# A pre-norm decoder layer: two pairs of FFN blocks by two levels of Winograd's products in the first pass, another order of the inner products, and the second pass's operands loaded together

## The chip, the cores and the metric

The kernel runs on one core of a Trainium2 chip. The metric is the device time of one launch in microseconds (us), for the kernel before the median of three runs. A profile of one execution accompanies it: for each instruction its engine, its start, its length and what ended the idle time ahead of it. The engines are named PE (TensorE, matrix products, with PEld for its weight loads), DVE (VectorE), ACT (ScalarE), POOL (GpSimd) and SP (SyncE, which here only issues DMAs).

## What is computed

Everything is float32. The input `x` holds 16 batches of 128 rows of 1024 numbers. Three residual steps follow one another:

```python
x = x + attention(layernorm(x))                # one head, d = 256
x = x + linear_attention(layernorm(x), ctx)    # 8 heads of 64
x = x + ffn(layernorm(x))
```

The change lies in the third:

```python
g = einsum('bsh,ih->bsi', x, Wg)     # 2048 rows x 1024 -> 2752
u = einsum('bsh,ih->bsi', x, Wu)
h = silu(g) * u
return einsum('bsi,hi->bsh', h, Wd)  # 2752 -> 1024
```

`Wg`, `Wu` and `Wd` come as packed 4-bit numbers with a scale and a zero for each group of 64; the kernel unpacks them itself.

## The kernel before

**One level.** The 2752 rows of gate and up are cut into ten blocks of 256 and a last one of 192. The 2048 rows of `x` are taken in two passes of 1024. For a block and a pass, a product of 256 x 1024 by 1024 x 1024 is cut into two by two in every dimension and made of Winograd's seven products instead of eight. Each of the seven, numbered 1 to 7, is four matmuls of 128 x 128 x 512. `one_block` (L1113) does seven for gate and seven for up, in the order `GATE` = 1, 7, 6, 2, 5, 4, 3 (L39). The left operands, the combined weights, come from DRAM; the right ones are the cut rows `T[1]` to `T[7]`.

**Two levels.** `two_levels` (L1295) takes two blocks, 2i and 2i+1, at once. For each of the seven outer products q, in the order `DOWN` = 1, 2, 6, 5, 3, 7, 4 (L40), it cuts the operands once more and does seven inner products p, each of four matmuls of 128 x 128 x 256. Four left combinations of an outer product (p = 7, 5, 6, 3) are made by GpSimd (`inner_left`, the tile `li`); four right ones (p = 7, 5, 6, 4) by VectorE (`inner_right`, the tile `ti`), each a subtraction of 128 x 512. The other operands are parts of `w` and `T[q]`. In the first pass a right combination is made for each outer product of each pair. In the second pass those of q = 1, 6, 5, 4, 7 are kept from the first pair on (`KEPT`, L1230), and q = 2 and 3 are made again in each pair.

**Sums.** Inner products 6, 5 and 3 add to the PSUM bank of product 1, and 4 to that of product 7. ScalarE copies the bank after 1, 7 and 6 (`k`). `got` (L1339) takes one quarter of an outer product out of PSUM: quarter (0,0) after product 2, (1,1) after 5, (1,0) after 4, (0,1) after 3, and adds it to the sums `U`, `V` and `C`. Quarters with a copy to add take two VectorE instructions (three for q = 7, one for q = 1), the last takes one (two for q = 7; for q = 1 a ScalarE copy). When a quarter of the pair's result is complete (q = 2, 3, 7, 4), `finish` (L1365) sets ScalarE to the SiLU of gate and leaves two VectorE products (`h`) for the next outer product, in `soon_due`.

**The order.** TensorE, VectorE and GpSimd run these parts in the order of the program text (`InOrder`, L54). The queues `right` (right combinations of the next outer product) and `extra` (combinations of the second pass's results) are worked off by `do_extra(n, more)` at fixed places. So the lines L1417 to L1461 are the order of every engine: before, one turn of the loop for outer product n had TensorE do n's 6, 2, 5, 4, then 1 of n+1, then n's 3, then 7 of n+1.

**Preparation.** `prepare` (L200) is a generator that unpacks the weights of blocks 5 to 10 and of `Wd`. One step unpacks half a matrix (two integer instructions and two float ones on VectorE, the tile `pa`) or makes four combinations (`pc`). SP loads the packed numbers (L173, L176, L192, L193) two halves ahead and stores the results (L209). `beside` (L1502) takes a number of steps after each one-level product, counted by its place n in the block; `two_levels` takes one after q = 1, 6 and 5 in the first pass; what is left is done after the last block (L1550).

**Weights and rows.** `load_weights` (L1012) keeps four tiles of two weight matrices each ahead of their use, on SP. In the first pass, blocks 0 to 5 go by one level, blocks 6 and 7 (pair 3) by two, then blocks 8 and 9 and the last block by one. The second pass does all five pairs by two levels. Its rows `T1` are loaded from DRAM by `block_loads` (L541) into memory that the two-level stage of the first pass leaves: eight loads of 512 KB on SP, one after every third product of blocks 8 and 9 (L1517). `outer_operand` (L1061) makes three right operands of the second pass during the first pass's last block, `last_block` (L1142).

Of the kernel before, what the change touches and what calls it, by code (L numbers as in the profile page):

```python
# [65 lines left out]
def decoder_layer(  # L66
# [474 lines left out]
    def block_loads(p, blocks):  # L541

        for k in ((0, 0), (1, 0), (1, 1), (0, 1)):
            for i in range(2):
                part = slice(None), ts(i, JC // 2)
                tc.keep_in_program_order(nc.sync.dma_start(blocks[k][part], xt_all[p][k][part]))
                yield
# [415 lines left out]
    with ExitStack() as gs:  # L963
# [36 lines left out]
            return [[(2 * i + f, mat, q) for mat in "gu"] for q in DOWN for f in range(2)]  # L1000


        PAIRS = [3]
        order = [blk for blk in range(RB) if blk // 2 not in PAIRS]
        order.insert(2 * PAIRS[0], None)
        to_load = deque([t for blk in order[: 2 * PAIRS[0]] for t in tiles_of(blk)])
# [288 lines left out]
        def two_levels(ps, pairs, operands, between=lambda q: None):  # L1295
# [9 lines left out]
            def do_extra(n, more=0):  # L1305
                for todo, k in ((right, n), (extra, more)):
                    for _ in range(min(k, len(todo))):
                        todo.popleft()()
# [5 lines left out]
            def multiply(n, p):  # L1314
                L, bank = state[n]["L"], state[n]["bank"]
                q = OUTERS[n][1]
                set_ = {6: 1, 5: 1, 3: 1, 4: 7}.get(p, p)
                if set_ == p:
                    bank[p] = banks[n % 2].tile([P, 2, HT], F32, name=f"q{p}", tag="gu")
                dst = bank[set_]  # L1320
                for m in range(2):
                    for c in range(CHUNKS):
                        tensor.matmul(
                            dst[:, m, :],
                            L[p][:, m, c, :],
                            R[q, p][:, c, :],

                            start=(set_ == p and m == c == 0),
                            stop=(p in (2, 3, 4) and c == CHUNKS - 1),
                            skip_group_check=True,  # L1330
                        )
                if p in (1, 7, 6):
                    t = state[n]["kept"][p] = ct.tile(
                        [P, 2, HT], F32, name="k", tag=f"k{p}", bufs=2 if p == 1 else 1
                    )
                    scalar.copy(t, dst)
                put_stores()

            def got(n, ib, p, add):  # L1339

                q = OUTERS[n][1]
                src = state[n]["bank"][p]
                add = state[n]["kept"].get(add)
                k = 2 * ib[0] + ib[1]
                add_to = vector.tensor_tensor
                U, V, C = (sums.get(x) for x in "UVC")
                if q == 1:
                    if add is None:
                        scalar.copy(U[:, k], src)
                    else:  # L1350
                        add_to(U[:, k], src, add, ALU.add)
                    return
                dst, base = {2: (C, U), 6: (U, U), 5: (V, U), 3: (C, V), 7: (C, V), 4: (C, U)}[q]
                if add is None:
                    if q == 7:
                        add_to(U[:, k], src, U[:, k], ALU.add)
                    add_to(dst[:, k], src, base[:, k], ALU.add)
                    return
                m = V if q == 5 else C
                add_to(m[:, k], src, add, ALU.add)  # L1360
                if q == 7:
                    add_to(U[:, k], U[:, k], m[:, k], ALU.add)
                add_to(dst[:, k], m[:, k], base[:, k], ALU.add)
# [47 lines left out]
            for n, (i, q) in enumerate(OUTERS):  # L1411
                last = n + 1 == len(OUTERS)
                if q in (1, 5):
                    sums["U" if q == 1 else "V"] = place.tile(
                        wide, F32, name="U" if q == 1 else "V"
                    )
                load_weights()  # L1417
                if not last:
                    prepare_outer(n + 1)
                    left = state[n + 1]["left"]  # L1420
                    left(7)
                multiply(n, 6)
                do_extra(len(right))
                while soon_due:
                    soon_due.popleft()()
                if q not in (1, 5):
                    sums["C"] = place.tile(wide, F32, name="C")
                if not last:
                    right.extend(operands.inner_right(OUTERS[n + 1][1]))
                if ps == 1 and n == 0:  # L1430
                    extra.append(lambda: outer_operand(operands.T, 4))
                elif ps == 1 and n == 4:
                    extra.extend(operands.inner_right(4))
                multiply(n, 2)
                got(n, (0, 0), 2, 1)
                multiply(n, 5)
                got(n, (1, 1), 1, 7)
                if not last:
                    left(5)
                    left(6)  # L1440
                do_extra(1, 1)
                multiply(n, 4)
                got(n, (1, 0), 7, 6)
                do_extra(1, 1)
                if not last:
                    multiply(n + 1, 1)
                    do_extra(1, 1)
                multiply(n, 3)
                got(n, (0, 1), 1, None)
                if not last:  # L1450
                    left(3)
                do_extra(0, 1)
                load_weights()

                do_extra(len(right) - 2)
                if not last:
                    multiply(n + 1, 7)
                    do_extra(len(right) - 1)
                if q in (2, 3, 7, 4):
                    finish(i, q)  # L1460
                between(q)  # L1461


                if ps == 0:
                    pass
                elif q == 3:
                    while extra:
                        extra.popleft()()
                    hl = load_first(i, 1)
                elif q == 7:  # L1470
                    soon_due.append(lambda i=i, hl=hl: combine(i, 1, hl))
                elif q == 1 and i > 0 or last:
                    while soon_due:
                        soon_due.popleft()()
                    do_extra(0, len(extra))
                    hl = load_first(i if last else i - 1, 0)
                    combine(i if last else i - 1, 0, hl)
                del state[n]
# [23 lines left out]
        def beside(n, mat, q):  # L1502
            if rest is None:
                tick()
                if not pend:
                    attention_done()
            else:

                if blk == 0:
                    steps = 1  # L1510
                elif blk == RB:
                    steps = n in (0, 2, 4)
                else:
                    steps = (1, 1 + (mat == "g" and blk < 3), 1, 0, 1, 0, 0)[n % 7]
                for _ in range(steps):
                    next(rest, None)
            if pass1 and n % 3 == 0:  # L1517
                next(pass1_loads, None)
            if blk == 2 * PAIRS[0] - 1 and n == 9:
                for step in first_operands.inner_right(DOWN[0]):  # L1520
                    step()

            if blk == RB:
                for k in {("r", 0): (5,), ("r", 1): (7,), ("m", 6): (6,)}.get((mat, q), ()):
                    outer_operand(T1, k)
                if (mat, q) == ("m", 1):
                    for step in second_operands.inner_right(1):
                        step()

        pass1 = None  # L1530
        for blk in order:
            if blk is None:
                two_levels(
                    0, PAIRS, first_operands, lambda q: q in (1, 6, 5) and next(rest, None)
                )
                deep.close()
                cxb = pool("c_xb", 1)
                pass1 = new_blocks(cxb, lambda k: f"b{k}")
                pass1_loads = block_loads(1, pass1)
                T1.update({1: pass1[0, 0], 2: pass1[1, 0], 3: pass1[1, 1]})  # L1540
                continue
            if blk == 2 * PAIRS[0] - 1:
                first_operands.pool = deep.enter_context(
                    tc.tile_pool(name="c_d", bufs=1, reuse_waits="tile")
                )
            one_block(blk, T, beside)
        blk = RB
# [282 lines left out]
```

## Time and profile before

| what | us |
|---|---|
| median of 3 runs (2287.0 to 2289.8) | 2288.38 |
| the profiled execution | 2287.6 |
| its span, first to last instruction | 2285.8 |
| TensorE busy in the span | 2258.2 |
| VectorE busy | 1600.1 |
| blocks 1 to 5, first pass, one level | 883.4 to 1123.75 |
| pair 3, first pass, two levels | 1123.75 to 1212.68 |
| blocks 8, 9 and the last one, one level | 1212.68 to 1346.58 |
| five pairs, second pass, two levels | 1346.58 to 1771.3 |

The times in the last four rows are places in the span. Each float32 matmul leaves two records, and a record's length overlaps with the next one's; what a stage costs is read from the start of its first record to the start of the next stage's first. `p` is the PSUM tile of a one-level product, `q` that of an inner product. An instruction made through `InOrder` carries the line of that helper, L62, so groups are told apart by the names of their tiles. The matmul records of product 4 are `q<-ti,w`, those of 5, 6 and 7 `q<-ti,li`, those of 3 `li` with `b` or `T`, those of 1 and 2 `w` with `b` or `T`.

### The profile page before, as it was taken

Reading aid. Unit: us, or ns where it says so; the run is one execution under the profiler, and the core shown is the slowest. Engines: PE = TensorE matmul, PEld = TensorE weight load, DVE = VectorE, ACT = ScalarE, POOL = GpSimd, SP = SyncE. Lnnn points to the kernel's source line nnn. Section 1 sums busy time; section 2 is a strip of 40 time slices with the busy share of each in tenths; the row PEclk is TensorE's granted clock in tenths of the full one; section 3 lists DMA queues with packets and bytes.
Section 4 is the critical chain, followed back from the end, with each engine's and each line's share of the span. In section 5 each row is a group of like instructions: output and inputs, shape, how many; then the busy total and the mean of one; then the engine's idle time right before and its main releaser. Section 6 shows DMA issues by size and latency. Waiting matters only on the chain.

```text
span 2285.8 us, 25587 instructions
## 1 busy us (share of the span) xinstructions
PE 2258.2 (99%) x9096; PEld 1612.5 (71%) x9096; DVE 1600.1 (70%) x2145; ACT 560.0 (24%) x893; POOL 471.8 (21%) x381
## 2 busy tenths in 40 slices
PE   8999999999999999999999999999999999999999
PEld 7556566666666664444584468888888588888888
DVE  6997788788788937666696658877777555544463
ACT  2111255665665652111111111121111100000000
POOL 5452122222222210000240024444443000000000
PEclk9999999999999999999999999999999999999999
DMA  6445366566676558877747942654554974434631
GB/s 246 158 135 182 102 166 183 158 194 185 173 230 196 169 165 269 276 261 262 242 137 232 322 137 95 202 185 139 192 196 137 331 242 151 142 124 149 222 116 37
DMA packets 270319, 425.23 MB, mean 186 GB/s; under 512 B 26224, under 2 KB 119792, under 8 KB 270064
## 3 DMA queue, kind: packets, MB, share of 16 engines
q1 hardware_dynamic: 244112, 377.71, 52.3%
q0 software_dynamic: 8064, 27.27, 3.2%
q10 hardware_dynamic: 18016, 18.62, 2.6%
q8 instruction: 73, 1.20, 0.2%
q14 instruction: 54, 0.44, 0.1%
HBM read 265.62 MB, written 157.35 MB: 185 GB/s over the span
## 4 chain that ended last, share of the span: by engine, by line
PE 91%; DVE 5%; issue 1%; DMA 1%; ACT 1%; POOL 0%; SPq 0%; DVEq 0%; POOLq 0%; ACTq 0%
PE po L1715 21%; PE q L62 20%; PE p L62 18%; PE mm L62 11%; PE kq L62 9%; PE mm L391 4%; PE tr L62 3%; PE mm L406 2%; PE p L1092 2%; DVE pa L62 1%; PE mm L287 1%; PE tr L338 1%; DVE ti L62 0%; DVE bnst L62 0%; DMA kh<-kd 0%
## 5 line engine op out<-in xcount | busy, mean ns | idle before, releaser
L62 PE MATMUL p<-b,w 128*128 128x512 f32 x560 | 246.4, 592 | 0.0
L62 PE MATMUL q<-ti,li 128*128 128x256 f32 x1008 | 232.2, 379 | 3.5 <-DVE ti L62 3.4
L62 PEld LDWEIGHTS q<-ti,li 128*128 128x128 f32 x1008 | 191.0, 190 | 31.3 <-issue 2.8
L62 POOL TENSOR_TENSOR li<-w 128x512 f32<-128x512 f32 x84 | 117.8, 1405 | 432.2 <-DMA w<-wu 244.4
L62 PEld LDWEIGHTS p<-b,w 128*128 128x128 f32 x560 | 106.4, 190 | 133.1 <-issue 129.4
L1715 PE MATMUL po<-wc,lc 128*128 128x256 f32 x840 | 183.4, 379 | 0.0
L62 PE MATMUL p<-T,w 128*128 128x512 f32 x400 | 177.2, 592 | 0.0
L709 POOL TENSOR_TENSOR qe<-qe,qden 128x1024 f32<-128x1024 f32 x64 | 121.7, 1901 | 266.5 <-DVE qden L62 244.7
L1715 PEld LDWEIGHTS po<-wc,lc 128*128 128x128 f32 x840 | 159.6, 190 | 21.8
L62 ACT COPY k<-q 128x512 f32<-128x512 f32 x126 | 73.7, 585 | 400.0 <-PE q L62 400.0
L62 PEld LDWEIGHTS p<-T,w 128*128 128x128 f32 x400 | 76.0, 190 | 95.7 <-issue 94.9
L1715 PE MATMUL po<-wq,lq 128*128 128x256 f32 x560 | 126.7, 379 | 0.4 <-issue 0.4
L62 PE MATMUL mm<-kh,cxt 128*128 128x256 f32 x512 | 122.6, 382 | 3.2 <-DMA kh<-kd 2.8
L62 PEld LDWEIGHTS mm<-qs,m_sb 128*128 128x128 f32 x512 | 97.2, 190 | 38.9 <-issue 28.0
L62 PE MATMUL kq<-cx,wk_sb 128*128 128x512 f32 x256 | 120.7, 594 | 3.5 <-ACT ke L666 3.5
L62 DVE TENSOR_REDUCE qmx<-kq 128x16 f32<-128x1024 f32 x64 | 76.3, 1193 | 63.8 <-PE kq L62 63.8
L62 PE MATMUL kq<-wq_sb,xn 128*128 128x512 f32 x256 | 120.4, 593 | 0.0
L62 PE MATMUL mm<-qs,m_sb 128*128 128x256 f32 x512 | 120.3, 379 | 0.0
L62 PEld LDWEIGHTS mm<-kh,cxt 128*128 128x128 f32 x512 | 95.9, 190 | 33.5 <-issue 19.1
L1715 PEld LDWEIGHTS po<-wq,lq 128*128 128x128 f32 x560 | 106.0, 190 | 16.0 <-issue 1.0
L62 DVE TENSOR_TENSOR pa<-pa,sz 128x1024 f32<-128x1024 int32 x86 | 114.6, 1333 | 2.5
L391 PE MATMUL mm<-xnT,wqkv_sb 128*128 128x512 f32 (+1 forms) x320 | 113.4, 511 | 0.0
(193 smaller groups left out, 3886.1 us busy)
## 6 DMA issues: line engine op xcount, KB each, us to landing
w<-wu SPq DMA_DIRECT2D x140, 256.0 KB, 3.1
lq<-h SPq DMA_DIRECT2D x140, 256.0 KB, 4.3
w<-wg SPq DMA_DIRECT2D x138, 256.0 KB, 2.8
kd<-kt SPq DMA_DIRECT2D x64, 512.0 KB, 3.5
kh<-kd SPq DMA_DIRECT2D x128, 256.0 KB, 5.6
h<-hc SPq DMA_DIRECT2D x80, 256.0 KB, 2.8
wq<-wd SPq DMA_DIRECT2D x70, 256.0 KB, 5.0
h<-h SPq DMA_DIRECT2D x60, 256.0 KB, 2.5
```

The costliest lines, as they stand in the source:

```text
L62: return lambda *args, **kw: self._tc.keep_in_program_order(fn(*args, **kw))
L287: tensor.matmul(ps, oT[:, d, ts(b % BPT, S)], wo_d[d][:, ts(h, 512)], start=(d == 0), stop=(d == 1),)
L338: nc.tensor.transpose(tr[:, j, :], xn[:, ts(4 * h + j, P)], ident)
L391: nc.tensor.matmul(ps[:, tokens], wqkv_sb[:, f, c, :], xnT[:, c, tokens], start=(c == 0), stop=(c == CC - 1),)
L406: nc.tensor.matmul(ps, xnT[:, c, ts(i, S)], wqkv_sb[:, 4:6, c, :], start=(c == 0), stop=(c == CC - 1),)
L709: nc.gpsimd.tensor_tensor(qe, qe, den.unsqueeze(2).to_broadcast(wide), ALU.mult)
L1092: tensor.matmul(ps, wt[:, j, :], T[q][:, j, :], start=(first == q and j == 0), stop=(q in (2, 3, 4) and j == JC - 1), skip_group_check=True,)
L1715: nc.tensor.matmul(bank[:, i, :], l[:, ts(i, S)], w,  start=(start and c == 0 and i % 2 == 0), stop=(stop and c == len(pairs) - 1), skip_g ...
```

## The change

Four edits stand in it. Blocks 8 and 9 are done by two levels too (`PAIRS`). Inside a turn of `two_levels` TensorE now does n's 2, 6, 4, 5, then 1 and 7 of n+1, then n's 3, and the calls of `got` and `do_extra` move with them. The preparation steps have other places: 11 in a full block, none in the second part of block 5, four in the last block. The eight loads of the second pass's rows are all issued after the pairs, and three right operands are made later in the last block.

```diff
-        PAIRS = [3]
+        PAIRS = [3, 4]
...
-                multiply(n, 6)
-                do_extra(len(right))
+                multiply(n, 2)
                 while soon_due:
                     soon_due.popleft()()
                 if q not in (1, 5):
                     sums["C"] = place.tile(wide, F32, name="C")
+                got(n, (0, 0), 2, 1)
+                do_extra(len(right))
+                multiply(n, 6)
                 if not last:
                     right.extend(operands.inner_right(OUTERS[n + 1][1]))
...
-                multiply(n, 2)
-                got(n, (0, 0), 2, 1)
+                multiply(n, 4)
+                got(n, (1, 0), 7, 6)
+                do_extra(1, 1)
                 multiply(n, 5)
                 got(n, (1, 1), 1, 7)
                 if not last:
                     left(5)
                     left(6)
                 do_extra(1, 1)
-                multiply(n, 4)
-                got(n, (1, 0), 7, 6)
-                do_extra(1, 1)
+
+                do_extra(len(right) - 3)
                 if not last:
                     multiply(n + 1, 1)
-                    do_extra(1, 1)
+                    do_extra(0, 1)
+                    multiply(n + 1, 7)
                 multiply(n, 3)
                 got(n, (0, 1), 1, None)
                 if not last:
                     left(3)
-                do_extra(0, 1)
+                do_extra(1, 1)
                 load_weights()
-
-                do_extra(len(right) - 2)
-                if not last:
-                    multiply(n + 1, 7)
-                    do_extra(len(right) - 1)
+                do_extra(len(right) - 1)
                 if q in (2, 3, 7, 4):
                     finish(i, q)
                 between(q)
...
                 elif blk == RB:
-                    steps = n in (0, 2, 4)
+                    steps = (2, 1, 1)[n] if n < 3 else 0
                 else:
-                    steps = (1, 1 + (mat == "g" and blk < 3), 1, 0, 1, 0, 0)[n % 7]
+                    steps = (1, 2, 1, 0, mat == "g", 0, 1)[n % 7]
+                    if blk == 2 * PAIRS[0] - 1 and n > 9:
+                        steps = 0
                 for _ in range(steps):
                     next(rest, None)
-            if pass1 and n % 3 == 0:
-                next(pass1_loads, None)
...
-                for k in {("r", 0): (5,), ("r", 1): (7,), ("m", 6): (6,)}.get((mat, q), ()):
+                for k in {("m", 7): (5,), ("m", 6): (7,), ("m", 2): (6,)}.get((mat, q), ()):
                     outer_operand(T1, k)
...
-                pass1_loads = block_loads(1, pass1)
+                for _ in block_loads(1, pass1):
+                    pass
```

More of the change, by code (lines that the diff above doesn't have):

```diff
@@ L1528, in beside @@
                         step()
-        pass1 = None
         for blk in order:
```

## Prediction

> **What bounds the kernel now.** I read the page's busy times first, then the chain that ended last, the busy times by stage, TensorE's waits, and last the timelines of the two-level stage. From the page, busy time of each engine over the span:
>
> ```profile
> PE 2258.2 (99%) x9096; PEld 1612.5 (71%) x9096; DVE 1600.1 (70%) x2145; ACT 560.0 (24%) x893; POOL 471.8 (21%) x381
> ```
>
> From the chain (start, length, what):
>
> ```profile
> 883.41 240.33 PE p L62 x560
> 1123.75 34.55 PE q L62 x160
> ```
>
> From the table by stage (stretch, its length, busy times, clock, DMA share, GB/s), and TensorE's waits (in all, times, longest):
>
> ```profile
> 883.40:931.50 48.10, 48.10 (x114) 21.31 (x113) 37.60 (x52) 7.26 (x11) 0.00 (x0) 1.00 0.93 308
> 979.50:1027.60 48.10, 48.10 (x114) 21.31 (x113) 30.63 (x42) 6.01 (x10) 0.00 (x0) 1.00 0.78 257
> 1123.75:1212.68 88.93, 85.62 (x393) 74.08 (x393) 75.25 (x91) 15.76 (x25) 35.13 (x24) 1.00 0.44 144
> 1260.70:1308.80 48.10, 48.10 (x114) 21.31 (x113) 29.91 (x42) 5.79 (x10) 0.00 (x0) 1.00 1.01 314
> 1346.60:1771.30 424.70, 424.00 (x1961) 372.02 (x1961) 323.22 (x406) 83.19 (x130) 181.48 (x136) 1.00 0.48 161
> ```
>
> ```profile
> PE q L62 <- DVE ti L62: 3.9, 5, 2.4
> ```
>
> TensorE sets the end: the one-level blocks run without a gap. A matmul leaves two records. A 512-column record takes 240.33/560 = 0.4292 us, a 256-column one 34.55/160 = 0.2159 us. One block is 14 products of 8 records, 112 x 0.4292 = 48.07 us. One pair by two levels is 7 outer products of 7 inner products of 8 records: an inner product is 1.727 us, an outer one 12.09 us, a pair 84.63 us. The pair of now (1123.75 to 1212.68) takes 88.93, so 4.3 us is waiting, on `ti`, VectorE's right operands. The second pass's five pairs take 424.7 for 423.2 of work: 1.5 us of waiting. So TensorE has little to gain, and VectorE, 75.25 busy of 88.93 in the pair, is close behind it.
>
> The same place in the timelines of TensorE and VectorE (start, length, instruction, count, wait before it):
>
> ```profile
> 1159.84 1.89 PE L62 MATMUL q<-T,li 128*128 128x256 f32 x8
> 1161.57 3.62 PE L62 MATMUL q<-ti,li 128*128 128x256 f32 x16
> 1165.02 1.89 PE L62 MATMUL q<-T,w 128*128 128x256 f32 x8
> 1166.75 1.89 PE L62 MATMUL q<-ti,li 128*128 128x256 f32 x8
> 1168.84 1.99 PE L62 MATMUL q<-ti,w 128*128 128x256 f32 x8 [0.20 <-DVE ti L62]
> ```
>
> ```profile
> 1161.77 0.69 DVE L62 TENSOR_TENSOR U<-q,U 128x512 f32<-128x512 f32 x1
> 1162.38 1.39 DVE L62 TENSOR_SCALAR pa<-raw 128x512 int32<-128x512 int32 x2
> 1163.80 4.38 DVE L62 TENSOR_TENSOR pa<-pa,sz 128x1024 f32<-128x1024 int32 x2
> 1168.10 0.68 DVE L62 TENSOR_TENSOR ti<-T,ti 128x512 f32<-128x512 f32 x1
> ```
>
> The reader is to see VectorE's order: the accumulation of product 3, a step of the weight preparation, then the right operand of product 4 (I call it R4). Product 4 (`q<-ti,w`) follows 3 by four products, 7', 6, 2, 5, that is by 6.91 us, and still waits.
>
> **What the skill says.** "TensorE: Matmul & The Clock Gate", Step-by-step, says that matmuls stay in program order and only weight loads are pulled ahead; so a late R4 stops everything behind product 4. No line here shows otherwise. "DVE: scalar operands, raw-bit mode, write accounting and state across instructions", section 5, calls VectorE's queue one in-order queue; the timeline above agrees. "SBUF — State Buffer", "SBUF: two separate sides", says that a VectorE instruction with two SBUF inputs and a GpSimd one that reads SBUF exclude each other for a whole instruction. The trace agrees: `ti<-b` takes 0.68 alone and 1.25 at 1133.10, where GpSimd's `li` holds until 1133.80; accumulations out of PSUM stay at 0.69.
>
> **The change, part by part.**
>
> *Blocks 8 and 9 by two levels.* 2 x 48.07 = 96.1 us of one-level work becomes 84.6: -11.5. GpSimd gains 28 `li` combinations of about 1.3 us (36 us), free in themselves since GpSimd does nothing else there; their price is what they add to VectorE, below. ScalarE gains some 16 us as in the pair of now, hidden. Weight loads and stores of results keep their number (28 and 8 of 256 KB).
>
> *The inner order.* Count from t = 0, the end of product 3 of the outer product before. Then TensorE did 7', 6, 2, 5, 4; now 7' has gone ahead of 3 and it does 2, 6, 4. R4's deadline moves from 6.91 to 3.45. VectorE did accumulation of 3, a preparation step if any, R4, the two `h` products if any, accumulation of 2. Now it does accumulation of 3, R6 (which stood ahead of 3 before), step or `h`, accumulation of 2, R4. So R4 moves behind two or three instructions that it did not wait for, and its deadline comes earlier. Wherever right operands are made, product 4 becomes the wait that ends last. Behind it stand all TensorE's later products; behind R4 on VectorE only accumulations that wait for product 4 themselves, so VectorE cannot work the delay off in advance. The pieces, from the timelines: lag to VectorE 0.27; an accumulation 0.69, two chained 1.40; R4 0.65; R6 1.25 because `li` 3 falls on it; `h` pair 2.36 to 2.50, take 2.45 (1.29 without GpSimd); SiLU 1.06 with 0.13 of hand-over; a unit step 4.2, 5.8 and 4.7 in the pair, take 4.7 (3.24 in the blocks, without GpSimd).
>
> - Quiet (after q = 1): 1.73 + 0.27 + 1.40 + 0.65 = 4.05, 0.6 late. A step of four combinations (2.75) fits ahead of it, for q = 1 has one instruction per accumulation.
> - Only accumulations (second pass, after q = 6 or 5): 0.27 + 0.69 + 1.25 + 1.40 + 0.45 (one meeting with GpSimd, as 1.13 for 0.69) + 0.65 = 4.7, 1.3 late.
> - `h` pair (after q = 2, 3, 7, 4): 0.27 + 0.69 + 0.13 + 1.06 + 2.45 + 1.40 + 0.65 = 6.65, 3.2 late; for q = 7 one accumulation more, 3.9; for q = 4 the same behind SiLU, 3.8; for q = 1 one fewer, 2.5.
> - Unit step (first pass, after q = 6 or 5): 0.27 + 0.69 + 1.25 + 4.7 + 1.40 + 0.65 = 8.96, 5.5 late.
>
> First pair, q = 2, 6, 5, 3, 7, 4: 0.6 + 3.2 + 5.5 + 5.5 + 3.9 + 3.8 = 22.5 (its first outer product is prepared in block 5). Second pair: the same and 2.5 for q = 1, 25.0. That replaces 4.3. Second pass, pair 0: 0.6 + 3.2 + 1.3 + 1.3 + 3.9 = 10.3 (q = 4 is made earlier, by `extra`); pairs 1 to 4 make only q = 2 and 3 again: 4 x 1.9 = 7.6. Together 17.9, replacing 1.5.
>
> *Preparation steps moved into blocks 1 to 5.* There are 67 steps; block 0 does 3. Blocks 1 to 5 did 42, now 54; the pairs did 3, now 6; the last block 3, now 4. A step is about 3.05 us (two of 3.24, one of 2.75 by turns). A full block's VectorE work becomes 11 x 3.05 + 6.9 = 40.5 of 48.1. The tightest place: five steps and the accumulations of 3 and 2 stand ahead of that of product 5: 15.5 + 0.7 + 1.4 brings its PSUM read to 18.3, and product 3 needs it by 20.6, 2.3 to spare. Block 1 shows that it goes: 37.60 busy and no gap. DMA: 257 GB/s at 8 steps, 308 at 10 make about 320 at 11, share 0.97; blocks 8 and 9 ran at 1.01 without a gap. SP carries these loads and stores beside the weights, which are four tiles (27 us) ahead. I take 0. If the raw loads come late, a waiting step holds an accumulation: up to +8.
>
> *Loads of the second pass.* Eight of 512 KB are issued together on SP after the pairs. They wait for the last `h` product (about 5 us), and then need 4.2 MB/300 GB/s = 14 us, all landed near 20. Queued behind them are the last block's fifth weight tile, needed at 34.3, and preparation loads and stores. The operand that needs the last block comes at 20.6; three operands of 2.3 us still end ahead of the accumulation of 5, which product 3 needs at 34.3. Cost 0; a landing after about 25 would be paid one for one.
>
> Sum: -11.5 - 4.3 - 1.5 + 47.5 + 17.9 = +48.1. Span 2285.8 + 48.1 = 2333.9; 1.8 lies around it (2287.6 the execution), and the median is 0.8 above that execution: 2336.5, say 2336.
>
> **Rivals.**
> - No meetings with GpSimd: `h` 1.29, step 3.24, R6 0.6. Classes 0.6, 0.6, 2.0, 3.4; pairs 14.7 + 16.0, second pass 11.3; -17.3 + 42.0 = +24.7, 2313. The 1.39 and 4.38 above speak against it, but GpSimd's instructions shift too.
> - DMA and SP decide: blocks 1 to 5 lose 8 and the last block 5, steps last 5.8: 2350 to 2360. For it: share 1.01 already. Against: no gap there.
> - Faster: each late R4 costs only the quiet 0.6, because the work ahead of it is done before product 2 ends. With 13 in each pass, 26 x 0.6 = 15.6, against 17.3 won: -1.7; under 0.66 per place it turns, at 0.4 it gives 2282. Against it, that work waits for product 3 itself.
>
> **How the numbers follow.** 0.2% (4.6 us) is what a measurement can tell from no change. Chances: forecast 0.66 (2322 to 2350), no meetings 0.16, DMA 0.12, the quiet case 0.06, half of it faster, half same. So 0.03, 0.03, 0.94. The range takes in the rival below and half of that above: 2310 to 2356.
>
> **What would show it.** TensorE's wait on `ti` grows from 3.9 to about 65 us, in front of `q<-ti,w`; `q` matmul records 2352 to 2744; two pairs 217 us; second pass 441; blocks 1 to 5 unchanged at 48.1. Wrong if product 4 does not wait, or waits under 0.7 us.

## The result and the profile after

The changed kernel takes 2361.02 us (median of 6 runs, 2358.99 to 2363.36), the kernel before 2288.61 in the same runs: a ratio of 1.0317, 95% interval 1.0304 to 1.033. Slower was forecast, but 2336 was too little, and the range ended at 2356. The profiled execution took 2360.97 us, its span 2358.8.

The page of the changed kernel, busy time of each engine, and its table by stage, cut at the same places as before: blocks 1 to 5, the two pairs, the last block, the second pass's pairs.

```profile
PE 2276.8 (97%) x9264; PEld 1658.9 (70%) x9264; DVE 1635.3 (69%) x2210; ACT 567.1 (24%) x899; POOL 514.8 (22%) x409
```

```profile
885.55:1135.99 250.44, 242.96 (x561) 107.53 (x561) 202.98 (x276) 31.25 (x51) 6.20 (x4) 0.98 0.97 311
1135.99:1363.67 227.68, 191.19 (x786) 158.23 (x785) 146.14 (x188) 33.16 (x51) 73.56 (x52) 0.93 0.35 115
1363.67:1401.43 37.76, 37.76 (x89) 16.75 (x89) 28.32 (x33) 5.25 (x8) 9.12 (x4) 1.00 0.77 263
1401.43:1844.46 443.03, 429.53 (x1962) 372.72 (x1961) 306.03 (x406) 85.06 (x130) 180.93 (x136) 1.00 0.46 156
```

The first column after the stretch is its length, the next TensorE's busy time, and the third from the end the granted clock. The reader is to see three things: blocks 1 to 5 are no longer without a gap; the two pairs take 227.68 for 169.3 of work; and there the clock is 0.93, where before it was 1.00 in every stage.

| stage | before | predicted | after | missed by |
|---|---|---|---|---|
| up to block 1 | 883.4 | 883.4 | 885.6 | +2.1 |
| blocks 1 to 5 | 240.3 | 240.3 | 250.4 | +10.1 |
| blocks 6 to 9 | 185.0 | 216.8 | 227.7 | +10.9 |
| last block | 37.8 | 37.8 | 37.8 | 0 |
| second pass, pairs | 424.7 | 441.1 | 443.0 | +1.9 |

The row for blocks 6 to 9 before is one pair, 88.9, and two blocks, 96.1. The first row is the same code in both kernels; over all runs of this study block 1 began between 883.4 and 886.4, so those 2.1 us are no effect.

One turn of the two-level stage, the one for q = 5 after q = 6, in the timelines of TensorE and VectorE:

```profile
1181.46 1.89 PE L62 MATMUL q<-T,w 128*128 128x256 f32 x8
1183.67 1.97 PE L62 MATMUL q<-ti,li 128*128 128x256 f32 x8 [0.32 <-DVE ti L62]
1189.10 3.53 PE L62 MATMUL q<-ti,w 128*128 128x256 f32 x8 [3.46 <-issue]
1192.42 2.06 PE L62 MATMUL q<-ti,li 128*128 128x256 f32 x8
```

```profile
1181.67 0.69 DVE L62 TENSOR_TENSOR U<-q,U 128x512 f32<-128x512 f32 x1 [2.66 <-PE q L62]
1182.27 1.25 DVE L62 TENSOR_TENSOR ti<-T,ti 128x512 f32<-128x512 f32 x1
1183.45 0.75 DVE L62 TENSOR_SCALAR pa<-raw 128x512 int32<-128x512 int32 x2
1184.24 2.49 DVE L62 TENSOR_TENSOR pa<-pa,szd 128x1024 f32<-128x1024 int32 x2
1186.64 0.68 DVE L62 TENSOR_TENSOR V<-q,k 128x512 f32<-128x512 f32 x1
1187.36 1.04 DVE L62 TENSOR_TENSOR V<-V,U 128x512 f32<-128x512 f32 x1
1188.32 0.68 DVE L62 TENSOR_TENSOR ti<-T,ti 128x512 f32<-128x512 f32 x1
```

It is the order that the prediction wrote down: accumulation of 3, R6, the step, accumulation of 2, R4. R4 ends at 1189.00, and product 4 starts at 1189.10. The profile puts this wait down to "issue", not to `ti`; only the times, and the run below that moves R4, show whose it is. What the prediction did not have: product 4 then takes 3.32 us (1189.10 to 1192.42) where a product takes 1.73. The table by stage, cut to single products:

```profile
1189.10:1192.40 3.30, 3.30 (x8) 2.63 (x9) 0.00 (x0) 0.00 (x0) 0.00 (x0) 0.54 0.24 53
1192.40:1194.30 1.90, 1.90 (x9) 1.67 (x8) 1.53 (x3) 0.00 (x0) 0.00 (x0) 0.91 0.34 38
1194.30:1196.00 1.70, 1.70 (x9) 1.51 (x8) 1.67 (x3) 0.00 (x0) 1.27 (x1) 1.00 0.98 357
```

Behind the wait the granted clock is 0.54, then 0.91, and only then 1.00.

The other new loss stands at the end of block 5, in the timelines of VectorE and TensorE:

```profile
1119.05 1.83 DVE L62 TENSOR_SCALAR pa<-raw 128x512 int32<-128x512 int32 x2 [3.39 <-DMA wd<-pa]
1120.92 4.37 DVE L62 TENSOR_TENSOR pa<-pa,szd 128x1024 f32<-128x1024 int32 x2
1125.21 1.28 DVE L62 TENSOR_TENSOR ti<-b 128x512 f32<-128x512 f32 x2
1126.53 1.42 DVE L62 TENSOR_TENSOR ti<-b,ti 128x512 f32<-128x512 f32 x2
1127.87 0.68 DVE L62 TENSOR_TENSOR h<-p,k 128x512 f32<-128x512 f32 x1
...
1129.19 0.68 DVE L62 TENSOR_TENSOR h<-p,k 128x512 f32<-128x512 f32 x1
```

```profile
1115.42 7.03 PE L62 MATMUL p<-T,w 128*128 128x512 f32 x16
1129.93 6.07 PE L62 MATMUL p<-b,w 128*128 128x512 f32 x8 [7.48 <-DVE h L62]
```

The step's first instruction waits 3.39 us for a store of earlier prepared weights to free its buffer, its float part takes 4.37 instead of 2.48 beside two of GpSimd's first four `li`, and the four `ti` stand behind it. The `h` that reads product 5's bank comes third in the row of waiting accumulations. Product 3 waits 7.48 us for it and then runs slow: 5.9 us, where a 512-column product takes 3.43.

### The profile page after: what moved, and what is told of

It reads as the page before. It is cut to its first block, busy times and chain, and to the rows that moved or that the text cites. A ratio compares the mean times of both kernels' runs of the same rounds, so it can differ in the third digit from the quotient of the medians.

```text
span 2358.8 us, 26048 instructions
## 1 busy us (share of the span) xinstructions
PE 2276.8 (97%) x9264; PEld 1658.9 (70%) x9264; DVE 1635.3 (69%) x2210; ACT 567.1 (24%) x899; POOL 514.8 (22%) x409
## 4 chain that ended last, share of the span: by engine, by line
PE 86%; DVE 7%; issue 3%; DMA 3%; ACT 1%; SPq 0%; POOL 0%; DVEq 0%; ACTq 0%; POOLq 0%
PE q L62 24%; PE po L1714 20%; PE p L62 12%; PE mm L62 11%; PE kq L62 8%; PE mm L391 4%; PE tr L62 3%; PE mm L406 2%; PE p L1092 2%; DVE pa L62 1%; DVE ti L62 1%; PE mm L287 1%; DMA szd<-in_dsz 1%; DMA kh<-kd 1%; PE tr L338 1%
## 5 line engine op out<-in xcount | busy, mean ns | idle before, releaser
L62 PE MATMUL q<-ti,li 128*128 128x256 f32 x1176 | 284.4, 386 | 8.2 <-DVE ti L62 8.2
L62 PEld LDWEIGHTS q<-ti,li 128*128 128x128 f32 x1176 | 227.1, 194 | 46.8 <-POOL li L62 12.8
L62 POOL TENSOR_TENSOR li<-w 128x512 f32<-128x512 f32 x98 | 134.9, 1378 | 440.0 <-DMA w<-wu 262.6
L62 ACT COPY k<-q 128x512 f32<-128x512 f32 x147 | 86.1, 585 | 499.8 <-PE q L62 499.8
L62 PE MATMUL p<-b,w 128*128 128x512 f32 x432 | 192.6, 599 | 7.5 <-DVE h L62 7.5
L62 PEld LDWEIGHTS p<-b,w 128*128 128x128 f32 x432 | 83.2, 193 | 111.5 <-issue 100.2
L62 PE MATMUL q<-ti,w 128*128 128x256 f32 x392 | 107.2, 423 | 39.7 <-issue 38.2
L62 PE MATMUL p<-T,w 128*128 128x512 f32 x304 | 134.7, 593 | 0.0
L62 PEld LDWEIGHTS q<-ti,w 128*128 128x128 f32 x392 | 79.9, 210 | 60.4 <-issue 46.8
L62 DVE TENSOR_TENSOR C<-q,k 128x512 f32<-128x512 f32 x105 | 72.2, 688 | 71.7 <-PE q L62 69.5
L62 PEld LDWEIGHTS mm<-kh,cxt 128*128 128x128 f32 x512 | 96.1, 190 | 33.5 <-issue 18.5
L1714 PEld LDWEIGHTS po<-wq,lq 128*128 128x128 f32 x560 | 106.3, 190 | 15.6 <-issue 1.1
```

The lines of the kernel that those rows point to most:

```text
L62: return lambda *args, **kw: self._tc.keep_in_program_order(fn(*args, **kw))
L1714: nc.tensor.matmul(bank[:, i, :], l[:, ts(i, S)], w,  start=(start and c == 0 and i % 2 == 0), stop=(stop and c == len(pairs) - 1), skip_g ...
```

## The experiments

All times are medians, of 2 to 20 runs, beside runs of the kernel before on the same chip; a ratio is to the kernel before, with its 95% interval.

**The order alone.** The body of the turn in `two_levels` of the changed kernel, put into the kernel before; nothing else.

```diff
-                multiply(n, 6)
-                do_extra(len(right))
+                multiply(n, 2)
...
+                got(n, (0, 0), 2, 1)
+                do_extra(len(right))
+                multiply(n, 6)
```

> The kernel before with the new inner order alone (one pair in the first pass, steps and loads as before). Theory: product 4 waits for its right operand, which the new order puts behind the accumulation of product 2. Then pair 3 gets about 29 us of waiting and slow records in place of 4.3 (+25), the second pass about 18 more: 2325 to 2335. Rival, that the second pair, the preparation steps or the DMAs made the loss: the order alone costs under 10 us, below 2299.

Measured: 2333.95 us, 1.0191 times the kernel before (1.0171 to 1.0211). Its table by stage, pair 3 and the second pass's pairs:

```profile
1124.55:1237.47 112.92, 95.19 (x394) 78.97 (x393) 69.80 (x91) 16.07 (x25) 35.28 (x24) 0.92 0.35 117
1371.37:1816.29 444.92, 431.43 (x1961) 372.85 (x1961) 307.55 (x406) 85.15 (x130) 181.12 (x136) 0.99 0.46 155
```

Pair 3 loses 24.0 us and the second pass 20.2. So the order is the main cause, and needs neither the second pair nor the new steps nor the loads together.

**The old order in the changed kernel.** The reverse: two pairs, new steps and loads, but the turn as before.

```diff
-                multiply(n, 2)
+                multiply(n, 6)
+                do_extra(len(right))
...
-                got(n, (0, 0), 2, 1)
-                do_extra(len(right))
-                multiply(n, 6)
```

> The changed kernel with the old inner order; two pairs, the new steps and the loads together stay. Theory: what is left is 11.5 us of TensorE work fewer, some 4 us of waiting in the second pair as in the first, and the 10 us that block 5 lost: 2288 to 2295, with blocks 1 to 5 still at 250 us. Rival, that two pairs after one another overload VectorE in any order: above 2310.

Measured: 2295.96 us, ratio 1.0022 (1.0013 to 1.003), one microsecond past the expected range. Of the 72 us that the change cost, some 65 are gone. The second pass's pairs take 425.0 again. Table by stage, blocks 1 to 5 and the pairs:

```profile
884.67:1132.28 247.61, 242.29 (x562) 106.97 (x561) 203.00 (x276) 31.28 (x51) 6.17 (x4) 0.99 0.97 314
1132.28:1313.94 181.66, 174.08 (x785) 150.14 (x785) 156.20 (x188) 32.58 (x51) 74.25 (x52) 0.98 0.44 144
```

The two pairs take 181.66 against 185.0 for the pair and two blocks: 3.3 us won of 11.5, because each pair waits, as the one before did, and because the matmuls behind one of these waits run slow (shown further below). Blocks 1 to 5 lose 7.3.

**R4 ahead of everything that delays it,** in the changed kernel: at the end of the turn before.

```diff
                 load_weights()
-                do_extra(len(right) - 1)
+                do_extra(len(right))
                 if q in (2, 3, 7, 4):
```

> The changed kernel with the right operand of product 4 made at the end of the turn before, ahead of the step, the h products and the accumulation of product 2. Theory: product 4 is no longer what waits longest; two pairs fall from 228 to about 190 to 200 us, the second pass from 443 to about 430: 2310 to 2325. Rival, that VectorE's work in a turn is too much wherever it stands: above 2345.

Measured: 2307.26 us, ratio 1.0074 (1.0054 to 1.0095): 54 us less than the changed kernel from one operand's place. The fall went past the expected range, 2310 to 2325: the pairs take 185.8 us and the second pass 430.4, and the clock in the pairs is 1.00. The pairs in the table by stage, and TensorE's waits in its products:

```profile
1137.26:1323.05 185.79, 173.50 (x785) 147.47 (x785) 146.13 (x188) 33.20 (x51) 72.08 (x52) 1.00 0.43 141
```

```profile
PE q L62 <- DVE ti L62: 15.4, 25, 1.8
```

The waits of 38.2 us that the profile of the changed kernel calls "issue" are gone with it. This shows that they were waits for R4; in the changed kernel's trace R4 ends 0.10 us before product 4 starts in each of the 18. Blocks 1 to 5 keep their loss (252.35).

**The wait filled,** to price the clock by itself. Four matmuls more ahead of product 4, in eleven turns of the pairs and two of the second pass, among them every turn where it waits 2.4 us or more; their result, in a PSUM tile of its own, is never read.

```diff
+                if (n > 0 and OUTERS[n - 1][1] != 1) if ps == 0 else n in (2, 5):
+                    fill = banks[n % 2].tile([P, 2, HT], F32, name="qf", tag="gu")
+                    for m in range(2):
+                        for c in range(CHUNKS):
+                            tensor.matmul(
+                                fill[:, m, :],
+                                state[n]["L"][2][:, m, c, :],
+                                R[q, 2][:, c, :],
+                                start=True,
+                                stop=True,
+                                skip_group_check=True,
+                            )
                 multiply(n, 4)
```

> The changed kernel with four more matmuls (1.7 us) ahead of product 4 wherever it waits for 2.4 us or more, into a PSUM tile that nobody reads. Theory, that the halved clock behind a wait costs time of its own: the operand comes when it came, the filled wait keeps the clock at 1.00, and 15 to 25 us go, 2336 to 2346. Rival, that the long records are only how a wait ends and VectorE sets the pace: no gain, or up to 15 x 1.7 = 26 us more, 2358 to 2387.

Measured: 2345.23 us, ratio 1.024 (1.022 to 1.0261): 16 us faster than the changed kernel (ratios 1.024 and 1.0317, intervals apart), with more work. The timeline of TensorE, the same turn as above, and the pairs in the table by stage:

```profile
1179.57 1.97 PE L62 MATMUL q<-ti,li 128*128 128x256 f32 x8 [0.32 <-DVE ti L62]
1181.37 1.89 PE L62 MATMUL qf<-T,w 128*128 128x256 f32 x8
1184.99 1.97 PE L62 MATMUL q<-ti,w 128*128 128x256 f32 x8 [1.73 <-issue]
```

```profile
1133.58:1347.38 213.80, 194.40 (x873) 163.75 (x873) 145.89 (x188) 33.16 (x51) 74.28 (x52) 1.00 0.37 123
```

The idle 3.46 has become 1.73 of filling and 1.73 idle: the operand comes when it came. But product 4 takes 1.80 (the next one starts at 1186.79), and the clock is 1.00. In the changed kernel TensorE's busy time in the pairs exceeds 0.2159 a record by 191.19 - 786 x 0.2159 = 21.5 us, here by 194.40 - 873 x 0.2159 = 5.9. These 5.9 are the edges of the gaps, where a record's length overlaps with no other; both kernels have 26 gaps of more than 0.15 us there. The difference, 15.6 us, is the slow clock. Of it 13.9 come back in the stage's length, 227.68 - 213.80; some is lost again where the four matmuls take longer than the wait was. Outside the pairs little moves: the second pass takes 441.5 for 443.0, the last block 39.8 for 37.8.

**The steps alone,** in the kernel before: the lines of `beside` that place the preparation steps.

```diff
-                    steps = n in (0, 2, 4)
+                    steps = (2, 1, 1)[n] if n < 3 else 0
                 else:
-                    steps = (1, 1 + (mat == "g" and blk < 3), 1, 0, 1, 0, 0)[n % 7]
+                    steps = (1, 2, 1, 0, mat == "g", 0, 1)[n % 7]
+                    if blk == 2 * PAIRS[0] - 1 and n > 9:
+                        steps = 0
```

> The kernel before with the new places of the preparation steps alone (one pair, old inner order, old loads). Theory: blocks 1 to 5 take 247 to 252 us instead of 240.3, all of it in block 5, nothing else moves: 2295 to 2302. Rival, that the loss in block 5 needs the second pair or the second pass's loads: 2288 to 2292.

Measured: 2300.61 us, ratio 1.0053 (1.0037 to 1.0068). Table by stage, blocks 1 to 4 and block 5:

```profile
884.37:1076.57 192.20, 192.20 (x450) 85.05 (x449) 157.94 (x218) 25.28 (x41) 0.00 (x0) 1.00 0.97 316
1076.57:1133.51 56.94, 50.95 (x114) 22.21 (x113) 45.01 (x58) 6.00 (x10) 6.16 (x4) 0.94 0.97 298
```

Four blocks with 11 steps each and a DMA share of 0.97 run without a gap, as predicted. All the loss is in block 5, 56.9 us where a block has 48.07 of work, and neither the second pair nor the loads are needed for it.

**One step fewer in block 5,** in the old order with two pairs.

```diff
-                    steps = (2, 1, 1)[n] if n < 3 else 0
+                    steps = (2, 2, 1)[n] if n < 3 else 0
...
-                    if blk == 2 * PAIRS[0] - 1 and n > 9:
+                    if blk == 2 * PAIRS[0] - 1 and n > 8:
```

> The kernel with the old inner order, two pairs and the new steps, but with the last preparation step of block 5 taken out (9 instead of 10) and done in the last block. Theory: block 5 lost its 7 us because that step waits for stores and meets GpSimd's first li, with three accumulations queued behind it; without it blocks 1 to 5 take 240 to 242 us and the whole 2287 to 2291. Rival, that the DMAs are overloaded over all five blocks: the wait moves to another step and blocks 1 to 5 stay above 245, the whole above 2293.

Measured: 2287.03 us, ratio 0.9986 (0.9979 to 0.9993). Blocks 1 to 5 in the table by stage, and VectorE's longest waits for DMAs in that stretch:

```profile
886.35:1126.69 240.34, 240.34 (x562) 106.41 (x561) 198.62 (x272) 31.28 (x51) 5.81 (x4) 1.00 0.98 315
```

```profile
DVE pa L62 <- DMA wu<-pa: 5.9, 2, 3.6
DVE pa L62 <- DMA szd<-in_dsz: 2.2, 2, 2.0
DVE pa L62 <- DMA wd<-pa: 1.5, 1, 1.5
```

VectorE still waits some 10 us for DMAs, up to 3.6 at a time, and TensorE loses nothing, at a DMA share of 0.98. So it is not the DMA load as such: a late step costs where it stands with no slack ahead of accumulations that TensorE needs. The step that was taken out both waited (3.39 us in the changed kernel) and ran long beside GpSimd (1.83 + 4.37 us); the run takes both away and does not tell them apart. It also leaves open why the store was late, whether by the DMA engines' share or by SP's order. A fourth buffer, or loads three ahead, might tell it, and was not tried.

**R4 early in the old order as well,** and block 5's `ti` two products later.

```diff
                     multiply(n + 1, 7)
-                    do_extra(len(right) - 1)
+                    do_extra(len(right))
...
-            if blk == 2 * PAIRS[0] - 1 and n == 9:
+            if blk == 2 * PAIRS[0] - 1 and n == 11:
```

> As the run with the lighter block 5, and the right operand of product 4 is made ahead of the step and the h products in the old inner order too, and the first right operands of the two-level stage two products later in block 5. Theory: the waits of 0.2 to 0.4 us ahead of product 4 go, that of 2.4 to 3.4 us after q = 7 stays or shrinks: 1 to 4 us below the run with the lighter block 5, 2284 to 2289. Rival: product 4 was no bottleneck in the old order and the later h products cost as much: no difference.

Measured: 2283.98 us, ratio 0.9975 (0.9966 to 0.9983): a quarter of a percent below the kernel before. Its pairs take 177.2 us instead of 178.6, and product 4 no longer appears among TensorE's waits. The gain lies in the waits after q = 7, which fall from 3.37 and 2.44 us to 2.10 and 1.48; two waits of 0.30 for R4 are gone, and two of some 0.75 for a copy `k` have come. Blocks 1 to 5 take 240.37 as without the two edits, so the place of block 5's `ti` changes nothing there.

## Why the prediction was right and wrong

**Right: what waits, where, and why.** R4 behind the accumulation of product 2, with an earlier deadline, was the mechanism. The order alone costs 44 us in its two stages, and moving R4 alone wins 54. The sign named in advance, 65 us of waiting for `ti`, came as 38.2 put down to "issue" and 8.2 to `ti`. The lateness of product 4, measured from t = 0 as in the prediction, against what was forecast:

| turn | forecast | measured in pair 3 or 4 |
|---|---|---|
| `h` pair (q = 6) | 3.2 | 1171.07 - 1164.46 - 3.45 = 3.2 |
| `h` pair, q = 7 | 3.9 | 1226.05 - 1218.84 - 3.45 = 3.8 |
| `h` pair, q = 4 | 3.8 | 1243.31 - 1236.44 - 3.45 = 3.4 |
| `h` pair, q = 1 | 2.5 | 1258.38 - 1253.71 - 3.45 = 1.2 |
| unit step (q = 5) | 5.5 | 1189.10 - 1181.46 - 3.45 = 4.2 |
| quiet (q = 2) | 0.6 | 1271.47 - 1267.09 - 3.45 = 0.9 |

The unit step was the term too large: taken at 4.7 us as it ran in the pair before, it took 3.2, since GpSimd's `li` now came to wait for VectorE (2.06 us at 1185.79, where it takes 1.27) instead of the other way round. For q = 1 the two `h` took 1.29 us, without GpSimd, where 2.45 had been taken. So product 4's lateness adds up to 39.8 us in the pairs, where 47.5 was forecast; with TensorE's other waits it is 227.68 - 191.19 = 36.5 us idle and 5.9 at the edges of the gaps, 42.4 in all.

**Wrong: "TensorE sets the end", with each record at its price.** The sum multiplied records by 0.2159 and added waits; it took the clock of 1.00 from the kernel before for granted. There the longest wait in the stage was 2.43 us. For ten waits of 2.0 to 3.5 us in the pairs it had to be asked what they do to the matmuls behind them, and the term was left out: 15.6 us of slow matmuls in the pairs, behind eight of the ten, where the waiting itself had been put 5.1 too high. That is nearly all of the +10.9 in the table, and the two errors hid part of each other. The Trainium skill, "TensorE: Matmul & The Clock Gate", What's actually happening, says that the array falls to half its clock after an idle window of about 3.4 us, and that these windows run freely, so that the moment of a change depends on where in a window the matmuls fall. The prediction used this page for the order of matmuls and not for this. The trace agrees in the half (0.54, 0.50) and in the chance: the same wait of 3.37 us for `ti` was followed by two products in 6.38 us in the run with the old order and by two in 3.53 in that with the lighter block 5. The first of these two products (start, length), in the one run and in the other:

```profile
1213.28 3.75 PE L62 MATMUL q<-ti,li 128*128 128x256 f32 x8 [3.37 <-DVE ti L62]
1207.58 1.97 PE L62 MATMUL q<-ti,li 128*128 128x256 f32 x8 [3.37 <-DVE ti L62]
```

It differs in the length: a wait of 2.42 (ahead of 1171.07) was followed by a clock of 0.76 and then 0.60, while one of 2.43 (ahead of 1286.79) kept 1.00. Over the nine profiles, in the two-level stages, no wait of 2.10 us or less is followed by slow matmuls, of nine waits of 2.42 to 2.44 us four are, and of those of 2.67 us and more all but that one of 3.37. One of the four stands in the run with the steps alone, ahead of 1213.57: the kernel before has the same wait of 2.43 us at the same place, and there the clock stayed at 1.00.

**Wrong: "I take 0" for the preparation steps.** The bound of +8 was named, with its mechanism, "if the raw loads come late, a waiting step holds an accumulation"; it was +10.1, and in the four other runs that keep all ten steps in block 5 and use new places +7.3 to +12.0. What came late was the store that frees a buffer, more than the raw loads. The step that failed was to work out the tightest place of a full block, which has 2.3 us to spare and in fact never failed, and not that of block 5, where four `ti` and GpSimd's first four `li` come in as well, and where the DMAs had been at a mean share of 0.97 for 190 us. Here too the slow clock added 2.5 of the 10.1, 5.90 for 3.43.

**The rivals.** "DMA and SP decide" had the places half right, block 5 alone, not all blocks, and not the last block. "No meetings with GpSimd" was right for the step, 3.24, but not for R6, which took 1.25 as before; its waits in the pairs, 14.7 + 16.0, were less than the 39.8 measured, and it left out the clock as well. "Faster" is out: no turn after a unit step or an `h` pair was late by less than 1.2.

**The rest held, in part by luck.** The second pass lost 18.3 for 16.4 forecast, but not from the terms of the sum: the turns with accumulations alone were 0.7 late instead of 1.3, while q = 7 was 5.6 late instead of 3.9 (product 6 waits 1.79 there first), and the clock behind that wait cost 1.6 more. The loads together and the later operands cost nothing: the last block takes 37.76 us in the changed kernel. What should be won, 11.5 us of TensorE work, is there: in the last run 177.2 for blocks 6 to 9 instead of 185.0, the other 3.7 lost to waits like those before.

## What to carry to other kernels

Where an operand is made on an in-order engine, put it ahead of everything there that waits for the consumer engine; asking "what stands before it, and what does that wait for?" gave the lateness to within 1.3 us in the pairs. Then ask what each wait does to what comes after it: here a wait of 2.4 us or more on TensorE could be paid again in slower matmuls. When work is moved into a stage with room on average, check the one place where other work joins it, not the average and not the regular place.

## What the runs showed that was not expected

The slow clock: in the pairs it held for some 3 to 6.5 us behind a wait, behind waits of some 2.4 us only in some cases, and filling the waits with four useless matmuls each made the kernel 16 us faster. And the profile named "issue" as what ended the waits for R4, 38.2 us in 18 places, so the largest loss did not stand under the name of its cause.
